# Two places and half transpositions for the planes of P, TensorE turns up to group 47, and an earlier load of x, in a macaron S4D block

## The chip, the cores and the metric

The kernel runs on one core of one Trainium2 chip. The metric is device time in microseconds (us) for one execution, the median of three runs. TensorE (PE) does the matmuls, VectorE (DVE), ScalarE (ACT) and GpSimd (POOL) the element-wise work, and SyncE (SP) issues most of the DMAs; ACT and POOL issue some too. Each engine works through its own queue in order.

## The reference

The input x is [8, 2048, 256] in float32: 8 sequences of 2048 tokens with 256 channels. A block of three sublayers is computed, each with a layer norm ahead of it and a residual after it:

```
x = x + 0.5 * ffn(layernorm(x))          # first feed-forward
x = x + s4d(layernorm(x))                # state-space convolution, with its own norm and skip
x = x + 0.5 * ffn(layernorm(x))          # second feed-forward, the same weights

ffn(v) = relu(v @ w1 + b1) @ w2 + b2     # 256 -> 1024 -> 256
K[h, l] = 2 Re sum_n Ct[h, n] exp(dtA[h, n] * l)      # 64 complex states for a channel
s4d(v) = layernorm(v + causal_conv(v, K) + v * D) * ln_w + ln_b
```

## The kernel before, in words

**Tiling.** The 16384 tokens are 128 blocks of 128, and two blocks make a group: there are 64 groups (`NG`). A feed-forward sublayer goes through the groups one after the other. Each group has eight slots (`SLOTS`), one for each 128 of the 1024 hidden channels. Values are split into a high and a low part, so in a slot `up` (L837) does six matmuls into `ph` and `down` (L848) six into `po`, the latter for the slot three before (`LAG`). Between them ACT takes the relu (L915) and DVE the low part (L916, shown as L116, since that is the helper's line). There are four buffers of `hx`.

**The order of the work.** `sublayer` (L862) counts steps t, one for each slot, from `-lead` on. In each step it writes the matmuls of a slot, and then calls `step()`, which advances every running generator by one `yield`. Generators are written as a number of yields before each action, so that the yields are the schedule. For group g, `pre` starts at step 8g - lead, and `post` at step 8g + 10. In `pre_a` (L966) the groups from 3 on load x into one of five slots of the tag `x` by a DMA that ACT issues (L971, pinned in ACT's order); the first three wait XL steps and load by SP. The statistics follow five steps after the load (`XY + 1`). The norm of a group's input and the norm of the output of the group three before are done together (`Joint`, L953).

**Turning the normalised tokens.** The first feed-forward matmul needs the channels on the partitions. Up to group 43 (`DMA_A = 44`) TensorE transposes four 128x128 blocks (L790), and ACT and DVE take the high and low part from PSUM (L799, L801). From group 44 on, `turn_by_dma` (L804) does it: DVE and ACT copy the low and the high 16-bit half of each number into two planes (L809), SP issues one DMA that transposes 16-bit blocks (L812), and DVE and ACT put the halves together again (L823), from which L825 and L827 take the high and low part. The planes, the turned planes and the result are tiles of the tag `pl`, which has two buffers of 2 KB for each partition.

**Making P in the background.** While the first sublayer runs, `matrices` (L257) makes the tables of the convolution as a background generator. It yields paces, and `fill` (L887) advances it whenever its sum of paces is behind the count of steps, of which each counts 1.32. The last part makes 32 tables P (`NBT`), each [128, 1024] in float32, in a pipeline of three parts, each with six sub-steps, over 9.1 units for the first 18 rounds and 10.3 after (`PA`, `PB_`):

- `make(bt)` (L586): six POOL operations write table bt.
- `spread(bt - 1)` (L612): in sub-steps 3 and 4, ACT copies the low and the high 16-bit halves of the table before into `planes` (L618); in sub-step 5, SP issues one DMA that transposes both planes, 16 blocks, into `turned` (L620); in sub-step 6 the table is stored as it is (L625).
- `transpose(bt - 2)` (L628): in sub-step 5, ahead of that DMA, DVE and ACT put the turned halves of the table before that together again (L635, `P_REINT`); in sub-step 6 the result is stored (L637).

So `planes` and `turned` are one place each: the copies of a table wait until the DMA of the table before has read `planes`, and the DMA waits until L635 has read `turned`. L618, L620 and L635 are pinned in the order of their queues.

**After the first sublayer.** The states are computed from P, scanned, and turned into outputs (`states`, `scan`, `outputs`), and the second feed-forward follows with the same code, in which all groups but two are turned by DMA (`DMA_B = 2`).

Of the kernel before, what the change touches and what calls it, by code (L numbers as in the profile page):

```python
# [13 lines left out]
U16 = mybir.dt.uint16  # L14
# [5 lines left out]
P = 128  # L20
# [23 lines left out]
def macaron_s4d_kernel(  # L44
# [17 lines left out]
    nc = tc.nc  # L62
    V = nc.vector
    A_ = nc.scalar
# [12 lines left out]
    TOK = NTB * P  # L77
    NG = NJ * B // NTB
    GPJ = B // NTB
    XL = 8  # L80
    LAGS_BEHIND = 3
    PIN = 1
    PINF = "a1", "a2"
# [2 lines left out]
    XY = 4  # L86
# [6 lines left out]
    BCH = 8  # L93
# [15 lines left out]
    def bank(tag, name):  # L109
        return ps.tile([P, 512], F32, name=name, tag=tag, bufs=BANKS[tag])  # L110

    def slot(tag, shape, name, dtype=F32):
        return work.tile(shape, dtype, name=name, tag=tag, bufs=BUFS[tag])

    def stt(o, a, s, b, op0, op1):
        return V.scalar_tensor_tensor(out=o, in0=a, scalar=s, in1=b, op0=op0, op1=op1)  # L116
# [19 lines left out]
    w1t, w2t = [wa1[:, i] for i in range(2)], [wa2[:, i] for i in range(2)]  # L136
# [15 lines left out]
    def load_weights():  # L152
        for _ in range(XL):
            yield
        pin = tc.keep_in_program_order
        q = W // 4
        raw1 = room[1][:, 0 : NDC * W].rearrange("p (i d f) -> p i d f", i=4, d=NDC)
        raw2 = room[1][:, NDC * W : NDC * W + NFC * H].rearrange("p (f m) -> p f m", m=H)
        at = NDC * W + NFC * H
        rows = [room[1][0:1, at + i * W : at + (i + 1) * W] for i in range(2)]  # L160
        ones = room[1][0:1, at + 2 * W : at + 2 * W + P]
        V.memset(ones, 1.0)
        nc.scalar.dma_start(out=rows[0], in_=w1[H - 1 : H])
        nc.scalar.dma_start(out=rows[1], in_=b1.rearrange("(o f) -> o f", o=1))

        spread_ = []

        def spread_rows(i):
            spread_.append([bank("ho"[i], f"spread{i}_{n}") for n in range(2)])
            for n in range(2):  # L170
                pin(nc.tensor.matmul(
                    spread_[i][n], ones, rows[n][:, i * 2 * q : (i + 1) * 2 * q],
                    start=True, stop=True,
                ))

        spread_rows(0)
        w2v = w2.rearrange("(fc p) m -> p fc m", p=P)
        for i in range(4):
            fs = slice(i * q, (i + 1) * q)
            W1Q[i].dma_start(  # L180
                out=raw1[:, i], in_=w1[:, fs].rearrange("(dc p) f -> p dc f", p=P)
            )
        for i in range(2):
            fs = slice(4 * i, 4 * i + 4)
            W2Q[i].dma_start(out=raw2[:, fs], in_=w2v[:, fs, :])
        for _ in range(7):
            yield
        for i in range(4):
            fs = slice(i * q, (i + 1) * q)
            hi = w1t[0][:, :, fs]  # L190
            last, bias = (b[:, i % 2 * q : (i % 2 + 1) * q] for b in spread_[i // 2])
            pin(V.tensor_sub(raw1[:, i], raw1[:, i], last.unsqueeze(1).to_broadcast([P, NDC, q])))
            pin(stt(raw1[:, i, NDC - 1], bias, ident[:, P - 1 : P], raw1[:, i, NDC - 1], ALU.mult, ALU.add))
            pin(A_.copy(hi, raw1[:, i]))  # L194
            pin(V.tensor_sub(w1t[1][:, :, fs], raw1[:, i], hi.bitcast(F32)))

            if i == 0:
                yield
                yield
                spread_rows(1)  # L200
            yield
        for i in range(4):
            fs = slice(2 * i, 2 * i + 2)
            hi = w2t[0][:, fs, :]
            pin(A_.activation(hi, raw2[:, fs], AF.Copy, scale=0.5))
            pin(stt(w2t[1][:, fs, :], raw2[:, fs], 0.5, hi.bitcast(F32), ALU.mult, ALU.subtract))
            yield
        for i in range(2):
            nc.sync.dma_start(out=w1_dram[i], in_=w1t[i].bitcast(F32))
            nc.sync.dma_start(out=w2_dram[i], in_=w2t[i].bitcast(F32))  # L210
# [46 lines left out]
    def matrices():  # L257
# [73 lines left out]
        f, a = r, z  # L331
# [29 lines left out]
        for k in range(1, 4):  # L361
# [14 lines left out]
        er, qr, qi, den, ta, tb, c2r, c2i, cr, ci, aa, ab, big, fa, fb, v, s, tt, g, e, mm_ = (  # L376
            cells[18:39]
        )
# [86 lines left out]
        for i in range(H // P):  # L465
            nc.gpsimd.dma_start(
                out=kpad[i * P : (i + 1) * P, P + 1 :], in_=zeros[:, 0 : P - 1]
# [6 lines left out]
        with nc.allow_non_contiguous_dma(reason="256 numbers"):  # L474
            nc.gpsimd.dma_start(
                out=kpad.rearrange("(g c) k -> c g k", c=2)[:, :, P], in_=k0
# [100 lines left out]
        def p_of(bt):  # L577

            r, i = (room[2], 28 + bt % 4 * 8) if bt < first else (room[3], (16, 24, 48, 56)[bt % 4])
            return r[:, i * P : (i + 8) * P]  # L580
# [31 lines left out]
        def spread(bt):  # L612

            pu = p_of(bt).bitcast(U16).rearrange("p (m w) -> p w m", w=2)
            yield
            yield
            for w in range(2):
                tc.keep_in_program_order(A_.copy(planes[:, w], pu[:, w]))  # L618
                yield
            tc.keep_in_program_order(nc.sync.dma_start(  # L620
                out=turned.rearrange("p w (k n) -> p (w k) n", n=P),
                in_=planes.rearrange("p w m -> p (w m)"), transpose=True,
            ))
            yield
            nc.sync.dma_start(out=o_dram[bt], in_=p_of(bt))  # L625
            yield
# [14 lines left out]
        planes, turned = both[:, 0], both[:, 1]  # L641
# [189 lines left out]
    XF = "pl"  # L831
    DEINT = (0, V.tensor_copy), (1, A_.copy)
    REINT = (0, V.tensor_copy), (1, A_.copy)
    DMA_A = 44
    DMA_B = 2

    def up(wt, xT, ph, fc):  # L837
# [125 lines left out]
    JG = 3  # L963
    P_MADE = 10, 46

    def pre_a(g):  # L966
        by_dma = g >= DMA_A
        for _ in range(XL if g < JG else 0):
            yield
        xt = xts[g] = slot("x", [P, NTB, H], f"xa_{g}")  # L970
        ins = (nc.scalar if g >= JG else nc.sync).dma_start(out=xt, in_=hbm(x, g))  # L971
        if g >= JG:
            tc.keep_in_program_order(ins)
        for _ in range(XY if g < JG else XY + 1):
            yield
        if g >= JG:
            joints[g - JG] = Joint(g - JG, by_dma)
        return (yield from ffn_in(xt, f"a{g}", NTB, by_dma, joints.get(g - JG)))
# [202 lines left out]
    def early():  # L1181

        xs = states_of(0)
        todo = list(batches(0))
        for j0, j1, pace in ((0, JE, 4.0), (JE, NJ - 1, 1.6)):
            while posted[0] < j1 * GPJ:
                yield 1.3
            n = (j1 - j0) * B
            per = min(512 // (2 * n), PB)
            for p0, bt in batches(0):  # L1190
                for l0 in range(0, PB, per):
                    pv = bank("b", f"pe{j0}_{bt}_{l0}")[:, 0 : 2 * per * n]
                    pv = pv.rearrange("p (r l m) -> p r l m", r=2, l=per)
                    for lb in range(l0, l0 + per, 2):
                        pts = []
                        for c in range(2):
                            pt = slot(("e", "te")[c], [P, 2, P], f"pe{bt}_{c}_{lb}_{j0}")
                            nc.sync.dma_start(
                                out=pt,
                                in_=pt_dram[bt].rearrange("k (c l m) -> k c l m", c=2, m=P)[:, c, lb : lb + 2],  # L1200
                            )
                            pts.append(pt)
                        yield pace
                        for l in range(lb, lb + 2):
                            for ri in range(2):
                                for c in range(2):
                                    nc.tensor.matmul(
                                        pv[c * N : (c + 1) * N, ri, l - l0, :],
                                        pts[c][:, l - lb, ri * N : (ri + 1) * N],
                                        some(j0, j1)[:, :, BCH * bt + 2 * l + c, :],  # L1210
                                        start=True, stop=True, skip_group_check=True,
                                    )
                        yield pace
                    keep(
                        xs, [pv[:, ri] for ri in range(2)], slice(p0 + l0, p0 + l0 + per),
                        slice((j0 + 1) * B, (j1 + 1) * B),
                    )
                    yield 1.3
            for _ in scan(0, G_, 0, sizes[0], max(j0, 1), j1, ("te", "e")):
                yield pace  # L1220
# [6 lines left out]
    def begin():  # L1227
        for _ in range(sizes[1] // PB):
            next(head)

    sublayer(
        w1t, w2t, pre_a, post_a, 19, "a", load_weights(), chain(matrices(), early()),
        {"half": NG // 2, "tables": NG * 3 // 4},
        {NG * SLOTS - 6: lambda: next(head), NG * SLOTS - 1: begin},
    )
# [126 lines left out]
```

## Time and profile before

| | |
|---|---|
| median of 3 runs | 1758.88 us (1758.41 to 1759.29) |
| the profiled execution | 1759.33 us, of which the span is 1757.4 us |
| busy: PE, DVE, ACT, POOL | 1723.9, 1378.7, 987.8, 587.8 us |
| first matmul of the states | 804 us |
| L618, copies into `planes` (ACT) | 64, 1046 ns at the median, from 221.1 to 580.7 us |
| L620, transposing DMAs of P (SP) | 32, landing 4.7 us after issue at the median |
| L635, copies out of `turned` | 32 on ACT of 1374 ns, 32 on DVE of 1285 ns at the median |
| L790, transposes of the first sublayer on PE | 176 |
| L812, transposing DMAs of the first sublayer | 20, landing 3.1 us after issue at the median |
| L971, loads of x by ACT | 61, landing 2.9 us after issue at the median |

How to read it: "L853 PE MATMUL po_a<-wa,hx_a" is an instruction of line 853 on TensorE that writes `po_a` from `wa` and `hx_a`; the suffix a is the first sublayer, b the second. A bracket behind an entry of a timeline is the time for which the engine was idle before it, and what ended that. In the rows of waits the three numbers are the total in us, the number of waits and the longest. In the windows each engine has its busy time and, in brackets, its instructions; behind them stand TensorE's granted clock (1.00 is full), the busy share of the DMA engines, and GB/s. In a tile's view three numbers with slashes are the shortest, the median and the longest duration in ns. SPq and ACTq are the queues of those engines, where DMAs are issued.

### The profile page before, as it was taken

What the parts mean: (1) busy time and instruction counts of PE and PEld (TensorE: products, weight loads), DVE (VectorE), ACT (ScalarE), POOL (GpSimd) and SP (SyncE); (2) the same over time, 40 slices, a digit from 0 to 9 for tenths busy, and PEclk for the clock granted to TensorE, in tenths of its full rate; (3) what the DMA queues carried; (4) which work ended last, traced back from release to release, by engine and by line L of the source; (5) the groups of instructions that cost most, each with busy time, mean ns of one, the idle gap of its engine ahead of it and who ended that gap; (6) DMA issues with size and microseconds to landing.
All of it is one profiled execution on the core that took longest, in us unless ns stands there. A gap on an engine that the chain in (4) does not pass through costs nothing.

```text
span 1757.4 us, 40914 instructions
## 1 busy us (share of the span) xinstructions
PE 1723.9 (98%) x15367; PEld 1696.8 (97%) x15367; DVE 1378.7 (78%) x4729; ACT 987.8 (56%) x2178; POOL 587.8 (33%) x550
## 2 busy tenths in 40 slices
PE   9999999999999999999999799999999999999998
PEld 7999999989999999999999799999999999999998
DVE  6998776676777767766999788888877888888884
ACT  4555476677777755544555445555455555555553
POOL 1117988886775105111000122222222222222220
PEclk9999999999999999999999999999999999999999
DMA  5111166566666533236888922222222222222321
GB/s 189 48 39 52 49 187 154 162 196 200 191 163 189 132 84 68 73 91 195 262 266 257 278 44 68 71 73 70 66 70 68 72 72 68 67 67 73 73 67 37
DMA packets 276861, 204.40 MB, mean 116 GB/s; under 512 B 162740, under 2 KB 235188, under 8 KB 276150
## 3 DMA queue, kind: packets, MB, share of 16 engines
q1 hardware_dynamic: 249232, 168.08, 35.6%
q10 hardware_dynamic: 26502, 32.52, 5.8%
q8 instruction: 120, 1.97, 0.5%
q0 software_dynamic: 928, 1.19, 0.4%
q14 instruction: 79, 0.65, 0.1%
HBM read 91.89 MB, written 71.57 MB: 93 GB/s over the span
## 4 chain that ended last, share of the span: by engine, by line
PE 71%; DVE 6%; DMA 4%; ACT 1%; issue 1%; POOL 0%; ACTq 0%; SPq 0%; DVEq 0%
PE ph_b L843 21%; PE po_b L853 21%; PE po_a L853 11%; PE ph_a L843 11%; PE pv L1089 2%; PE py L1164 2%; PE py L1155 2%; DMA planes<-planes 2%; DMA xa<-in_L_attn_x_dram 1%; DVE e L1119 1%; DVE te L1120 1%; DVE xsB L1122 1%; DMA pt<-pt 1%; DVE xsB L1121 1%; PE pt_a L790 0%
## 5 line engine op out<-in xcount | busy, mean ns | idle before, releaser
L853 PE MATMUL po_a<-wa,hx_a 128*128 128x256 f32 x3072 | 454.4, 285 | 11.9 <-DVE hx_a L116 11.9
L843 PE MATMUL ph_a<-xh_a,wa 128*128 128x256 f32 x2048 | 456.9, 287 | 0.7 <-ACT xh_a L799 0.7
L843 PE MATMUL ph_b<-xh_b,wb 128*128 128x256 f32 x2048 | 443.5, 284 | 0.7 <-ACT xh_b L799 0.7
L853 PE MATMUL po_b<-wb,hx_b 128*128 128x256 f32 x3072 | 441.6, 283 | 0.0
L853 PEld LDWEIGHTS po_a<-wa,hx_a 128*128 128x128 f32 x3072 | 405.1, 192 | 14.5 <-DVE hx_a L116 12.9
L853 PEld LDWEIGHTS po_b<-wb,hx_b 128*128 128x128 f32 x3072 | 401.1, 192 | 0.0
L843 PEld LDWEIGHTS ph_a<-xh_a,wa 128*128 128x128 f32 x2048 | 355.6, 193 | 3.8 <-ACT wa L194 1.5
L843 PEld LDWEIGHTS ph_b<-xh_b,wb 128*128 128x128 f32 x2048 | 353.3, 193 | 1.3 <-ACT xh_b L799 1.1
L915 ACT ACTIVATE hx_b<-ph_b 128x256 fp32r<-128x256 f32 x512 | 190.9, 383 | 259.6 <-PE ph_b L843 237.8
L915 ACT ACTIVATE hx_a<-ph_a 128x256 fp32r<-128x256 f32 x512 | 193.7, 387 | 228.5 <-PE ph_a L843 211.1
L116 DVE SCALAR_TENSOR_TENSOR hx_a<-ph_a,hx_a 128x256 fp32r<-128x256 f32 x512 | 208.9, 414 | 122.6 <-ACT hx_a L915 121.0
L843 PE MATMUL ph_a<-xl_a,wa 128*128 128x256 f32 x1024 | 290.6, 285 | 0.0
L843 PE MATMUL ph_b<-xl_b,wb 128*128 128x256 f32 x1024 | 285.5, 284 | 0.0
L116 DVE SCALAR_TENSOR_TENSOR hx_b<-ph_b,hx_b 128x256 fp32r<-128x256 f32 x512 | 210.1, 413 | 64.0 <-ACT hx_b L915 60.5
L1297 POOL TENSOR_TENSOR xb<-xb,lnb_sb 128x512 f32<-128x512 f32 x64 | 82.8, 1296 | 466.8 <-DMA xb<-x_dram 146.9
L843 PEld LDWEIGHTS ph_a<-xl_a,wa 128*128 128x128 f32 x1024 | 197.6, 193 | 0.6 <-DVE xl_a L801 0.4
L843 PEld LDWEIGHTS ph_b<-xl_b,wb 128*128 128x128 f32 x1024 | 197.7, 193 | 0.0
L773 POOL TENSOR_TENSOR xa<-xa,hb 128x512 f32<-128x512 f32 x64 | 85.0, 1328 | 288.0 <-ACT xn L726 283.8
L773 POOL TENSOR_TENSOR xb<-xb,hb 128x512 f32<-128x512 f32 x64 | 94.3, 1473 | 90.7 <-issue 58.7
L726 ACT ACTIVATE xn<-xb,nb_fb,t_fb 128x255 f32<-128x255 f32 x127 | 69.4, 594 | 89.0 <-DVE nb_fb L116 88.9
L726 ACT ACTIVATE u<-xa,nb_u,t_u 128x256 f32<-128x256 f32 x104 | 90.0, 865 | 0.0
L809 DVE COPY pl_b<-xn 128x512 uint16<-128x512 uint16 x62 | 27.1, 438 | 74.7 <-ACT xn L726 74.7
(266 smaller groups left out, 2553.3 us busy)
## 6 DMA issues: line engine op xcount, KB each, us to landing
o<-u SPq DMA_DIRECT2D x32, 512.0 KB, 4.0
pt<-u SPq DMA_DIRECT2D x32, 512.0 KB, 4.2
tz<-kpad SPq DMA_DIRECT2D x64, 256.0 KB, 4.6
xb<-x_dram SPq DMA_DIRECT2D x64, 256.0 KB, 2.7
out_dram<-xb SPq DMA_DIRECT2D x64, 256.0 KB, 2.9
x_dram<-xa ACTq DMA_DIRECT2D x62, 256.0 KB, 2.1
xa<-in_L_attn_x_dram ACTq DMA_DIRECT2D x61, 256.0 KB, 2.9
pt<-pt SPq DMA_DIRECT2D x60, 256.0 KB, 3.8
```

Source lines behind the costliest of these rows:

```text
L116: return V.scalar_tensor_tensor(out=o, in0=a, scalar=s, in1=b, op0=op0, op1=op1)
L726: ins = A_.activation(dst, src, AF.Identity, bias=nb[:, i : i + 1], scale=rs[:, i : i + 1])
L773: return G_.tensor_add(xt, xt, hb2.unsqueeze(1).to_broadcast([P, NTB, H]))
L809: copy(pl[:, w], xu[:, :, :, :, w])
L843: nc.tensor.matmul(ph, wt[wp][:, dc, fs], xp[:, dc, :], start=(n == 0), stop=(n == 3 * NDC - 1))
L853: nc.tensor.matmul(po[:, i, :], hp[:, tsl], wt[wp][:, fc, :], start=(fc == 0 and i == 0 and n == 0), stop=(fc == NFC - 1 and n == 2), skip ...
L915: last[A_] = A_.activation(hh, ph, AF.Relu)
L1089: ins = nc.tensor.matmul(pv[ri][c * N : (c + 1) * N, l, j0 * B : j1 * B], pts[c][:, l, ri * N : (ri + 1) * N], some(j0, j1)[:, :, BCH * bt ...
L1119: E.tensor_mul(t1, xv[:, :, :, j, :], wr_b)
L1155: nc.tensor.matmul(py[c][:, l, :], ucs[c][:, l, :], tzs[c][:, l, :], start=(l == 0), stop=False, skip_group_check=True,)
L1164: nc.tensor.matmul(py[c][:, l, :], xs[cs, ri, p0 + l, :], ots[ri][cs, l, :], start=False, stop=(l == PB - 1 and ri == 1), skip_group_check ...
L1297: G_.tensor_add(xt, xt, lnb_sb.unsqueeze(1).to_broadcast([P, NTB, H]))
```

## The change

Four things are changed.

- The planes of P lie in two places by turns. An even table uses `planes` as before; an odd table uses two half tiles of the tag `pl`, one for each plane.
- Each plane is turned by a DMA of its own, so that a table has two transposing DMAs of 8 blocks instead of one of 16. `turned` stays one tile, of which each DMA writes one half.
- `DMA_A` goes from 44 to 48: groups 44 to 47 of the first sublayer are turned by TensorE. As the tables are made by then, the tag `pl` isn't used by both.
- `lead` of the first sublayer goes from 19 to 20, XL from 8 to 9 and the yields behind a load from `XY + 1` to `XY + 2`: from group 3 on, the load of x stands one step earlier in ACT's order, and the statistics stand where they were.

```diff
-    XL = 8
+    XL = 9
...
             pu = p_of(bt).bitcast(U16).rearrange("p (m w) -> p w m", w=2)
+
+            if bt % 2:
+                halves_ = [slot("pl", [P, BCH * P], f"half{bt}_{w}", U16) for w in range(2)]
+            else:
+                halves_ = [planes[:, w] for w in range(2)]
             yield
             yield
             for w in range(2):
-                tc.keep_in_program_order(A_.copy(planes[:, w], pu[:, w]))
+                tc.keep_in_program_order(A_.copy(halves_[w], pu[:, w]))
                 yield
-            tc.keep_in_program_order(nc.sync.dma_start(
-                out=turned.rearrange("p w (k n) -> p (w k) n", n=P),
-                in_=planes.rearrange("p w m -> p (w m)"), transpose=True,
-            ))
+            for w in range(2):
+                tc.keep_in_program_order(nc.sync.dma_start(
+                    out=turned[:, w].rearrange("p (k n) -> p k n", n=P),
+                    in_=halves_[w], transpose=True,
+                ))
...
-    DMA_A = 44
+    DMA_A = 48
...
-        for _ in range(XY if g < JG else XY + 1):
+        for _ in range(XY if g < JG else XY + 2):
...
-        w1t, w2t, pre_a, post_a, 19, "a", load_weights(), chain(matrices(), early()),
+        w1t, w2t, pre_a, post_a, 20, "a", load_weights(), chain(matrices(), early()),
```

## The prediction

> **What bounds the kernel now.** I read the busy shares and the 40 slices first, then TensorE's waits, its timeline around each wait, the windows of 20 us for the same stretch, and last the waits of ScalarE (ACT) and the tile view of the planes.
>
> ```profile
> PE 1723.9 (98%) x15367; PEld 1696.8 (97%) x15367; DVE 1378.7 (78%) x4729; ACT 987.8 (56%) x2178; POOL 587.8 (33%) x550
> ...
> PE   9999999999999999999999799999999999999998
> ```
>
> TensorE is the bound, so an added matmul costs its full time, and a stall elsewhere counts only once it reaches TensorE. In the first sublayer that happens through one door; the waits give us in total, times, longest:
>
> ```profile
> PE po_a L853 <- DVE hx_a L116: 11.9, 9, 2.9
> ```
>
> ```profile
> 287.48 0.74 PE L853 MATMUL po_a<-wa,hx_a 128*128 128x256 f32 x4 [1.51 <-DVE hx_a L116]
> ...
> 341.77 0.98 PE L853 MATMUL po_a<-wa,hx_a 128*128 128x256 f32 x6 [1.84 <-DVE hx_a L116]
> 349.42 0.98 PE L853 MATMUL po_a<-wa,hx_a 128*128 128x256 f32 x6 [1.22 <-DVE hx_a L116]
> ...
> 394.62 0.98 PE L853 MATMUL po_a<-wa,hx_a 128*128 128x256 f32 x6 [2.92 <-DVE hx_a L116]
> ...
> 580.34 0.97 PE L853 MATMUL po_a<-wa,hx_a 128*128 128x256 f32 x6 [1.77 <-DVE hx_a L116]
> ```
>
> The bracket is the idle time. The other four are at 305.27 (0.53), 356.47 (0.95), 358.51 (0.35) and 566.84 (0.78). All nine lie between 280 and 600 us, most of the stretch in which P is made (221 to 594 us). Each has a tail: the first six po_a after it take 0.98 us where six take 0.72 in the chain, so 0.26 x 9 = 2.3 us. The longest one also costs clock:
>
> ```profile
> 340.00:360.00 20.00, 15.72 (x125) 15.09 (x125) 13.73 (x45) 15.56 (x29) 13.35 (x15) 1.00 0.78 200
> ...
> 380.00:400.00 20.00, 17.08 (x131) 16.88 (x130) 13.57 (x40) 13.61 (x24) 18.38 (x15) 0.91 0.82 222
> 400.00:420.00 20.00, 20.00 (x169) 20.00 (x168) 13.72 (x55) 17.05 (x30) 11.63 (x10) 1.00 0.75 228
> ```
>
> PE busy and its count stand second, the granted clock next to last but two. A clock of 0.91 over 20 us is 1.8 us lost. So 11.9 + 2.3 + 1.8 = 16.0 us. The counts say the same: against 170 matmuls in a full window, the seven short ones lack 14 + 7 + 2 + 45 + 39 + 23 + 6 = 136, at 20/170 = 0.118 us each 16.0 us. **That is all that this change can win.**
>
> What is behind the nine? ScalarE and VectorE (DVE) run in order, and while one waits at a P copy, the relus that feed TensorE stand behind it.
>
> ```profile
> ACT planes L618 <- DMA planes<-planes: 19.7, 15, 3.6
> ...
> ACT u L635 <- DMA planes<-planes: 4.1, 3, 2.2
> ```
>
> ```profile
> 337.79 1.99 ACT L618 COPY planes<-u 128x1024 uint16<-128x1024 uint16 x2 [3.64 <-DMA planes<-planes]
> ```
>
> ```profile
> 337.81 1.32 DVE L635 COPY u<-planes 128x1024 uint16<-128x1024 uint16 x1 [3.12 <-DMA planes<-planes]
> ...
> 578.21 0.75 DVE L675 BATCH_NORM_STATS2 st_fa<-xa 128x6 f32<-128x256 f32 x2 [3.90 <-DMA xa<-in_L_attn_x_dram]
> ```
>
> The chain of waits names the transfers (start, duration):
>
> ```profile
> 331.13 6.56 DMA planes<-planes
> ...
> 570.48 7.71 DMA xa<-in_L_attn_x_dram
> ```
>
> By the last wait ahead of each: five stalls hang on the planes' transposition (305.27, 341.77, 349.42, 356.47, 358.51: 4.89 us), three on x (287.48, 566.84, 580.34: 4.06 us), and 394.62 (2.92 us) on both, first 1.59 us of ACT at L635, then x, whose issue stood behind that.
>
> **The change, part by part.**
>
> *Two places.* L618 waits because the transposition of the batch before still reads `planes`. With places by turns it needs the one two batches back. A batch takes 9.1/1.32 of a step's time: a group with TensorE turns lasts 374.75 - 362.79 = 11.96 us, 1.495 a step, so 10.3 us up to the 18th batch (10.3/1.32 steps, 11.7 us, after). The largest landing is 8.8 us, so all 15 waits go (19.7 us of ACT). The odd halves take the tag `pl`, which no other tile uses until group 48. What is late next is L635, which still waits for its own transposition, and `turned` still has one place. But L635 of a batch comes two sub-steps of 10.3/6 after the L618 that stopped, 3.4 us, about the longest wait of 3.64.
>
> *Halves.* A half has the shape of the transposition of a group:
>
> ```profile
> L620 SPq DMA_TRANSPOSE planes<-planes x32: 1317/2028/4379, 223.2 to 583.3; - x32
> ...
> DMA to landing us min/median/max: 4.3/4.7/8.8
> ```
>
> ```profile
> L812 SPq DMA_TRANSPOSE pt_a<-pl_a x20: 1232/1232/1292, 551.9 to 778.8; - x20
> ...
> DMA to landing us min/median/max: 3.0/3.1/4.5
> ```
>
> The first half can be issued after the first copy of 1.05 us and lands in 3.1: 4.7 + 1.05 - 3.1 = 2.6 us sooner for VectorE's copy. The second is issued 1.23 later and lands 4.3 after the first: 1.4 us sooner for ScalarE's. The price is 2 x 1.23 - 2.03 = 0.43 us of SyncE's queue in each batch, hidden: queued behind on SP are only the stores of o and pt, which no engine waits for at that point (x is issued by ACT). If crowding stretches an issue to the row's 4.38, the second half lands up to 4.38 - 1.23 = 3.2 us later than so reckoned, 1.8 later than now. I take the median rows, since a half is the nearest shape, and keep the other end for the range.
> The Trainium skill speaks against this part: "DMA: Bandwidth & Descriptors", "Rules for kernel authors", says to coalesce small transfers, and its fit (in "Anatomy of one DMA") has about 2.0 us fixed for each. By that the second half would land some 2 us after the whole one, the stalls at 341.77, 356.47, 358.51 and 394.62 would stay (6.06 + 4 x 0.26 + 1.8 = 8.9 us), and the sum below would be some 1759 us. The rows (3.1 for half, 4.7 for all) show 1.6 us for the second half instead.
>
> *x a step sooner.* A step is 12 matmuls, 1.44 us in the chain. Reading, `lead` 19 to 20 and XL 8 to 9 cancel for the first three groups and the weights (steps -11, -3, 5; -11), and XY + 2 leaves the statistics where they were. What moves is one ACT-issued DMA per group (0.39 us of queue), now ahead of the store of the group before instead of just after it (570.08 and 570.48). Its slot was last read by the normalisation two steps before, so it should add no wait. Each of the three x stalls shrinks by at most 1.44: 1.44 + 0.78 + 1.44 = 3.66. An issue comes sooner only if ACT gets there, so I take 2.6. Below nothing is possible if x now meets the transposition, as at 279.25, where one issued 1.9 us earlier goes with a landing of 7.08; that end goes into the range.
>
> *Groups 44 to 47 by TensorE.* 16 more transposes. Periods: 11.96 with them, 597.87 - 586.35 = 11.52 by DMA. So 4 x 0.44 = **1.76 us added**, certain since nothing hides it. Gone are four transpositions from SP and, per group, 0.62 + 0.77 us on ACT and 0.68 + 0.45 less xl's equal share on DVE, just where 566.84 and 580.34 stall.
>
> **Sum.** Of the planes' five I take 4.5 of 4.89, of 394.62 2.2 of 2.92 (its ACT wait of 1.59 by the half's 1.4, its x by the step), of x's 2.6: 9.3 us. Seven tails 1.8, the clock 1.8: 12.9 won. Against it 1.76, and for the L635 waits that now end last two stalls of the present mean (11.9/9 + 0.26 = 1.6): 3.2. Net 7.9. The profiled execution took 1759.33 (span 1757.4 and 1.9 around it), giving 1751.4; it lies 0.45 above the median 1758.88, so **1751**.
>
> **The rivals.**
> *The wait moves.* L618's wait reappears at L635, because `turned` has one place and the transposition itself is no shorter; only x and its three stalls gain (2.6 + 0.8), less 1.76: about 1757. For it: 12.2 us of DVE waits at L635 already, 8 of them. Against: both halves come sooner. That the change does nothing lies here too: the copies are pinned in ACT's order, and if that order puts them no earlier, the freed place is unused.
> *Halves crowd the queues (slower).* Place: between 280 and 400 us, with DMA shares of 0.5 to 0.8. If an issue takes 4.4 us as the row's longest does, a batch is L635 (1.4) + 4.4 + 4.7 = 10.5 us, and from 10.3 on the copies fall behind in every batch. One stall of 1.6 in ten of the first 18 batches is 16, with 1.76, and 6 of the old ones cured: about 1771. Against: the issue's median of 2.03 for the whole.
>
> **Chances.** Forecast (1745 to 1755.4) 0.68, the wait moves (1755.4 to 1762.4) 0.16, slower 0.16. A measurement of this kernel can tell about 0.2% (3.5 us) from no change. Low end: all 16.0 won less 1.76 gives 1744.7. High end: 1762, where the crowded queue begins; some 0.03 lie below and 0.13 above.
>
> **What would show it.** Right: L618 has no waits on the DMA; po_a's waits fall from 11.9 to 2 to 5 us; no clock below 1.00 at 380 to 400; pt_a by TensorE has 192 transposes; a planes half lands in some 3 us. Wrong: DVE's and ACT's waits at L635 above their 16.3 us together, x landings above 7 us still ahead of st_fa, new po_a waits after 400 us, where there are none to 560.

## The result, and the profile after

The changed kernel takes 1764.17 us (median of 13 runs, 1759.88 to 1768.63), the kernel before beside it 1757.09 us (13 runs, 1754.20 to 1763.05): a ratio of 1.0035 with a 95% interval of 1.0024 to 1.0045. It is slower, by 6 us by the ratio and 7 by the medians, where 8 us less were forecast. The profiled execution took 1762.85 us, its span is 1760.7 us, 3.3 more than before, so the two traces show half of the loss. Lines behind L614 have moved down by five or six: L618 is now L623, L620 L626, L635 L641, L853 L859, L971 L977.

The busy time of TensorE and its slices, from the page of the changed kernel:

```profile
PE 1724.7 (98%) x15383; PEld 1696.4 (96%) x15383; DVE 1375.5 (78%) x4721; ACT 983.1 (56%) x2170; POOL 591.2 (34%) x550
...
PE   8999999999999999999999899999999999999998
```

TensorE has 16 instructions more, the transposes of groups 44 to 47, and still bounds the kernel. Its waits and those of its suppliers (total, times, longest):

```profile
DVE st_fa L681 <- DMA xa<-in_L_attn_x_dram: 32.3, 33, 3.2
ACT xn L732 <- DVE nb_u L119: 21.2, 17, 3.1
...
PE po_a L859 <- DVE hx_a L116: 9.5, 11, 2.1
...
ACT u L641 <- DMA planes<-planes: 6.0, 3, 2.8
...
DVE u L641 <- DMA planes<-planes: 3.1, 1, 3.1
```

Three of these rows before the change:

```profile
DVE st_fa L675 <- DMA xa<-in_L_attn_x_dram: 29.3, 33, 3.9
...
DVE u L635 <- DMA planes<-planes: 12.2, 8, 3.1
...
ACT xn L726 <- DVE nb_u L119: 9.1, 11, 1.4
```

ACT's 19.7 us at the copies into the planes have no row left at all. DVE's wait for its own transposition fell from 12.2 to 3.1 us, and 1.3 more for a half. But ACT's normalisation `xn` now waits 21.2 us for DVE's shift `nb_u`, where it was 9.1 us. The prediction doesn't speak of that row. The windows of 20 us of the changed kernel (PE busy and its count stand second, the clock next to last but two):

```profile
20.00:40.00 20.00, 19.10 (x154) 18.24 (x152) 13.38 (x56) 8.81 (x23) 1.27 (x1) 1.00 0.66 251
40.00:60.00 20.00, 17.44 (x141) 16.81 (x142) 15.46 (x59) 10.76 (x24) 3.87 (x3) 1.00 0.13 41
140.00:160.00 20.00, 17.93 (x149) 17.37 (x148) 19.35 (x45) 9.58 (x23) 17.91 (x21) 1.00 0.19 41
...
340.00:360.00 20.00, 18.01 (x145) 17.26 (x144) 16.20 (x56) 15.79 (x26) 15.89 (x16) 1.00 0.88 256
...
380.00:400.00 20.00, 20.00 (x170) 20.00 (x169) 14.33 (x59) 16.77 (x31) 16.23 (x15) 1.00 0.82 229
```

The stretch that the prediction looked at is better: 340 to 360 lacks 25 matmuls instead of 45, and 380 to 400 none, at full clock. But the first three windows held 159, 167 and 167 before. Counted as the prediction counted, against 170 matmuls in every window and at 0.118 us each, with the first `pv` (the first matmul of the states) beside it:

| profiled execution | lacking 20 to 220 us | lacking 220 to 600 us | first `pv` | `pv` to second feed-forward | the rest |
|---|---|---|---|---|---|
| before | 21 | 139 | 804.0 | 207.2 | 746.2 |
| after | 75 (+6.4 us) | 95 (-5.2 us) | 805.6 | 209.9 | 745.1 |
| without the x part (below) | 22 (+0.1 us) | 53 (-10.1 us) | 796.3 | 210.8 | 745.4 |

Up to the first `pv` the changed kernel loses 6.4 and gains 5.2 by these counts, which hold what the clock costs, and the 16 transposes are 1.8 us of added work: 3.0 us in all, where 1.6 were measured. (In the last row 10.0 less 1.8 makes 8.2 won, and 7.7 arrive at the first `pv`.) So the count is good to some 1.5 us, and the loss has two sides: the start, in which nothing of P is made, became worse, and the stretch of P gained half of what it gains without the earlier load of x.

**The first three groups.** SyncE's queue in the changed kernel:

```profile
4.36 1.43 SPq L977 DMA_DIRECT2D xa<-in_L_attn_x_dram  x1
20.44 1.06 SPq L209 DMA_DIRECT2D w_dram<-wa  x2
22.03 2.10 SPq L210 DMA_DIRECT2D w_dram<-wa  x2
24.18 1.24 SPq L977 DMA_DIRECT2D xa<-in_L_attn_x_dram  x1
```

The load of group 2 stands behind four stores of the weights. Before, it was the second of an entry of two, ahead of them:

```profile
4.36 3.18 SPq L971 DMA_DIRECT2D xa<-in_L_attn_x_dram  x2
```

DVE and TensorE pay for the late load (the timelines of both after the change):

```profile
35.08 0.75 DVE L681 BATCH_NORM_STATS2 st_fa<-xa 128x6 f32<-128x256 f32 x2 [1.62 <-DMA xa<-in_L_attn_x_dram]
```

```profile
40.04 0.33 PE L796 MATMUL pt_a<-ident,xn 128*128 128x128 f32 x1 [0.26 <-ACT xn L732]
40.53 0.55 PE L796 MATMUL pt_a<-ident,xn 128*128 128x128 f32 x3 [0.16 <-ACT xn L732]
41.75 0.74 PE L849 MATMUL ph_a<-xh_a,wa 128*128 128x256 f32 x4 [0.67 <-ACT xh_a L805]
44.17 0.38 PE L849 MATMUL ph_a<-xl_a,wa 128*128 128x256 f32 x1 [1.69 <-DVE xl_a L807]
```

Issued at 24.18, the load is there at 35.05, 10.87 us later. TensorE idles step by step as the late group reaches it: transposes, high part, low part. The windows 20 to 60 lack 31 matmuls more than before, 3.7 us.

**The statistics.** One place some 490 us on, as DVE, ACT and TensorE show it:

```profile
525.95 0.17 DVE L703 RECIPROCAL t_u<-s_u 128x4 f32<-128x4 f32 x1
528.48 0.75 DVE L681 BATCH_NORM_STATS2 st_fa<-xa 128x6 f32<-128x256 f32 x2 [2.36 <-DMA xa<-in_L_attn_x_dram]
...
531.23 0.58 DVE L119 TENSOR_SCALAR nb_u<-mv_j,t_u 128x1 f32<-128x1 f32 x4
```

```profile
531.48 1.09 ACT L732 ACTIVATE xn<-xa,nb_u,t_u 128x255 f32<-128x255 f32 x2 [3.11 <-DVE nb_u L119]
```

```profile
529.97 0.98 PE L859 MATMUL po_a<-wa,hx_a 128*128 128x256 f32 x6 [0.59 <-DVE hx_a L116]
```

`t_u` and `nb_u` belong to one group's norm, `st_fa` to the next group, whose x has only just been asked for. It stands in the middle of that norm, DVE waits 2.36 us for x with `nb_u` (and an `hx_a`) queued behind it, and ACT waits 3.11 us. By the order of DVE's instructions in the traces, `st_fa` of the next group is ahead of `nb_u` in 13 of 60 groups before, and in 45 of 60 after.

### The profile page after: what moved, and what is told of

Same layout as the page of the kernel before. It is cut to its first block, busy times and chain, and to the rows that moved or that the text cites. A ratio compares the mean times of both kernels' runs of the same rounds, so it can differ in the third digit from the quotient of the medians.

```text
span 1760.7 us, 40998 instructions
## 1 busy us (share of the span) xinstructions
PE 1724.7 (98%) x15383; PEld 1696.4 (96%) x15383; DVE 1375.5 (78%) x4721; ACT 983.1 (56%) x2170; POOL 591.2 (34%) x550
## 3 DMA queue, kind: packets, MB, share of 16 engines
q0 software_dynamic: 928, 1.19, 0.4%
## 4 chain that ended last, share of the span: by engine, by line
PE 89%; DMA 4%; DVE 3%; ACT 1%; issue 1%; SPq 0%; ACTq 0%; DVEq 0%
PE po_b L859 21%; PE ph_b L849 21%; PE po_a L859 18%; PE ph_a L849 18%; PE py L1170 3%; PE py L1161 3%; PE pv L1095 3%; DMA xa<-in_L_attn_x_dram 2%; PE pt_a L796 1%; DVE u L641 1%; DMA planes<-half 1%; DMA planes<-planes 1%; DMA pt<-pt 1%; DMA wb<-w_dram 1%; DVE hx_a L116 0%
## 5 line engine op out<-in xcount | busy, mean ns | idle before, releaser
L859 PE MATMUL po_a<-wa,hx_a 128*128 128x256 f32 x3072 | 455.6, 285 | 9.6 <-DVE hx_a L116 9.5
L859 PE MATMUL po_b<-wb,hx_b 128*128 128x256 f32 x3072 | 441.3, 283 | 0.5 <-DVE hx_b L116 0.5
L859 PEld LDWEIGHTS po_a<-wa,hx_a 128*128 128x128 f32 x3072 | 404.9, 192 | 12.9 <-DVE hx_a L116 12.2
L859 PEld LDWEIGHTS po_b<-wb,hx_b 128*128 128x128 f32 x3072 | 400.5, 192 | 1.0 <-DVE hx_b L116 0.9
```

The source lines that it names most:

```text
L859: nc.tensor.matmul(po[:, i, :], hp[:, tsl], wt[wp][:, fc, :], start=(fc == 0 and i == 0 and n == 0), stop=(fc == NFC - 1 and n == 2), skip ...
```

## The experiments

**Theory.** The parts on the planes do what was reckoned. The x part loses more than they win, in two ways: group 2 is loaded late, and the planner, which orders DVE's unpinned instructions, draws the statistics forward behind the earlier load. The second way was added after the first four runs below, whose expectations speak of the late group 2 alone. **Rivals:** the halves crowd the queues; turning groups 44 to 47 costs more than priced; an earlier load collides with the transpositions as such. Each kernel was timed in five rounds beside the kernel before, whose median in the four sessions was 1758.58 (the first four runs), 1758.03 (the next four), 1758.50 (the next four) and 1757.34 us. 0.001 in a ratio is 1.76 us; the intervals are some 2 us to either side, so differences of 1 to 3 us between two experiments are told by their medians alone. Where two experiments of different sessions are compared below, the times are not corrected for the 1.5 us by which the medians of the kernel before differ.

**Only the x part.** In the kernel before:

```diff
-    XL = 8
+    XL = 9
...
-        for _ in range(XY if g < JG else XY + 1):
+        for _ in range(XY if g < JG else XY + 2):
...
-        w1t, w2t, pre_a, post_a, 19, "a", load_weights(), chain(matrices(), early()),
+        w1t, w2t, pre_a, post_a, 20, "a", load_weights(), chain(matrices(), early()),
```

> Only the load of x a step sooner (lead 20, XL 9, XY + 2); planes in one place, turned whole, group 44 the first turned by DMA. Theory 'late group 2': group 3's load now stands a step ahead of group 2's, and so SyncE issues group 2's load behind the four stores of the split weights; it lands some 10 us after issue, and TensorE loses 4 to 6 us before 60 us of the span. So 3 to 6 us slower than the kernel before. Rival 'halves crowd the queues': this kernel has none of it, 1 to 3 us faster. Rival 'TensorE turns and what the planner makes of them': not here either, 1 to 3 us faster.

Measured 1776.34 us, 1.0105 (1.0092 to 1.0118). This alone loses 17.8 us, more than the whole change, and three times what the late group 2 was expected to cost.

**Everything but the x part.** The change, with these three edits taken back (XL 8, XY + 1, lead 19):

```diff
-    XL = 9
+    XL = 8
```

> Two places, halves and group 48, without the earlier load of x. 'Late group 2': no stall before 60 us, the stalls by the planes are mostly gone; 1 to 4 us faster than before. 'Halves crowd the queues': 4 to 10 us slower, with waits at the copies out of the turned planes. 'TensorE turns and the planner': 2 to 5 us slower, lost after 800 us of the span.

Measured 1752.97 us, 0.9969 (0.9957 to 0.9981): 5.6 us faster than before, more than was expected, and 11.2 less than the change. The waits of this kernel:

```profile
DVE st_fa L681 <- DMA xa<-in_L_attn_x_dram: 32.5, 37, 2.9
...
ACT xn L732 <- DVE nb_u L119: 7.5, 10, 1.4
...
PE po_a L859 <- DVE hx_a L116: 2.7, 6, 0.8
```

DVE waits for x about as often and as long as in the changed kernel (32.5 and 32.3 us), and TensorE hardly notices. What differs is what stands behind the wait. One such wait in DVE's timeline, first in this kernel, then in the one with the x part alone (the statistics that wait, and the shift of the group before them):

```profile
411.46 0.58 DVE L119 TENSOR_SCALAR nb_u<-mv_j,t_u 128x1 f32<-128x1 f32 x4
413.77 0.75 DVE L681 BATCH_NORM_STATS2 st_fa<-xa 128x6 f32<-128x256 f32 x2 [1.73 <-DMA xa<-in_L_attn_x_dram]
```

```profile
414.83 0.75 DVE L681 BATCH_NORM_STATS2 st_fa<-xa 128x6 f32<-128x256 f32 x2 [3.03 <-DMA xa<-in_L_attn_x_dram]
...
418.81 0.58 DVE L119 TENSOR_SCALAR nb_u<-mv_j,t_u 128x1 f32<-128x1 f32 x4
```

Shift first, and TensorE idles 0.19 us at 415.10. Statistics first, and it idles 1.73 us at 416.03. The count of groups with the statistics first is 14 of 60 here, 44 with the x part alone.

**Group 2 back in its place,** in the whole change. Groups 0 to 2 load one step sooner, so that group 2 is again not behind group 3:

```diff
-        for _ in range(XL if g < JG else 0):
+        for _ in range(XL - 1 if g < JG else 0):
...
-        for _ in range(XY if g < JG else XY + 2):
+        for _ in range(XY + 1 if g < JG else XY + 2):
```

> The whole change, but the first three groups wait XL - 1 steps and have XY + 1 yields behind the load, so that group 2's load stands ahead of group 3's again and SyncE issues it ahead of the weight stores. 'Late group 2': 4 to 6 us faster than the changed kernel, so 0 to 4 us faster than before. 'Halves crowd the queues' and 'TensorE turns and the planner': as slow as the changed kernel, 5 to 8 us slower than before.

Measured 1762.24 us, 1.0021 (1.0008 to 1.0033). The window 40 to 60 has its 167 matmuls again, but the gain is only 1.9 us where 4 to 6 were expected, and in the profiled execution the first `pv` comes later, at 809.0. So the late group 2 isn't the main cause. Statistics first: still 46 of 60.

**Only the groups 44 to 47,** in the kernel before:

```diff
-    DMA_A = 44
+    DMA_A = 48
```

> Only groups 44 to 47 turned by TensorE. By the 16 transposes 1.8 us slower than before, less up to 2.5 us for the two stalls at 566 and 580 us that the DMA turns took part in: between 1 us faster and 2 us slower by 'late group 2' and by 'halves crowd the queues'. 'TensorE turns and the planner': 3 to 6 us slower, with the loss after 800 us of the span.

Measured 1758.92 us, 1.0005 (0.9997 to 1.0014). This rival falls: 0.3 us, transposes and what they cure together.

**The statistics pinned,** in the whole change, in DVE's order at the place where the program has them:

```diff
-            stats(halves(xt), f"f{name}", mv=joint.mv[:, 0:NTB])
+            stats(halves(xt), f"f{name}", True, joint.mv[:, 0:NTB])
```

> The whole change, with the statistics of a joint group's x pinned in DVE's order at the place where the program has them (six steps behind the load, and behind the shift nb_u of the group before). Theory 'statistics ahead of the shift': the planner put them one or two slots behind the earlier load, ahead of nb_u of the group before in 45 of 60 groups (13 before the change), so DVE's wait for x delays nb_u, ACT's xn and the relus behind it; pinned, DVE's waits for x (32.3 us) and ACT's for nb_u (21.2 us) fall below 10 us, and the kernel is 6 to 11 us faster than the changed one, 1753 to 1758; the late load of group 2 is still there. Rival 'an earlier load collides on the DMA queues or in ACT's order': the waits for x stay and the time stays at 1761 to 1766.

Measured 1756.40 us, 0.9992 (0.9982 to 1.0002), where the change is at 1.0035. Its waits:

```profile
ACT xn L732 <- DVE nb_u L119: 7.4, 9, 1.8
...
DVE st_fa L681 <- DMA xa<-in_L_attn_x_dram: 4.1, 2, 2.6
```

With no group's statistics ahead of the shift, ACT's row is back at 7.4 us. This one word in the program is worth 7.8 us by the medians. Of the 6.1 us between the profiled executions, 2.9 lie ahead of the first `pv` and 2.9 behind it, in a stage that the pin doesn't touch (more on that at the end of the next section).

**Pinned, and group 2 in its place** (both edits above):

```diff
+        for _ in range(XL - 1 if g < JG else 0):
...
+            stats(halves(xt), f"f{name}", True, joint.mv[:, 0:NTB])
```

> The same, and group 2's load ahead of group 3's as in the third experiment. 'Statistics ahead of the shift' and the late group 2 as a second, smaller cost: 2 to 4 us faster than with the pin alone, 1749 to 1755, faster than the kernel before. Rival 'an earlier load collides': 1759 to 1764.

Measured 1754.99 us, 0.9985 (0.9976 to 0.9993), the upper end of what was expected, and 1.4 us below the one before where 2 to 4 were expected.

**Pinned, without the x part,** which asks whether the pin is a gain in itself:

```diff
-    XL = 9
+    XL = 8
...
+            stats(halves(xt), f"f{name}", True, joint.mv[:, 0:NTB])
```

> Two places, halves and group 48, the load of x where it was, and the statistics pinned. 'Statistics ahead of the shift': DVE's waits for x (32.5 us without the pin) nearly vanish; 0 to 4 us faster than the second experiment, 1749 to 1753. Rival 'an earlier load collides': the pin changes nothing, 1753.

Measured 1761.86 us, 1.0019 (1.0009 to 1.0029): a miss. That the pin is no gain in itself was expected, a loss of 8.9 us was not. One thing that it adds is a wait of ACT's root:

```profile
ACT s_u L692 <- DVE mv_j L685: 15.2, 19, 4.1
```

Without the pin it is 2.6 us in 3 waits. But the whole change with the same pin has this wait too, 15.0 us in 20 waits, and is 5.5 us faster than this kernel, so it isn't shown as the cause. What differs more between the two is ACT's wait at the copies L641, 14.0 us here and 7.8 there, the longest of 5.34:

```profile
369.34 1.33 ACT L641 COPY u<-planes 128x1024 uint16<-128x1024 uint16 x1 [5.34 <-DMA planes<-half]
```

How the pin and the later load bring that about was not tried.

**One place, halves and groups 44 to 47,** without the x part:

```diff
+            halves_ = [planes[:, w] for w in range(2)]
...
-    XL = 9
+    XL = 8
```

> Halves and group 48, but the planes in one place, the load of x where it was. If the second place is what frees ACT, ACT's waits at the copies into the planes stay near half of their 19.7 us (the halves come 1.6 to 2.6 us sooner) and the time lies between 1755 and 1758; if the halves alone do it, 1753 as in the second experiment; if the halves cost and the places pay, 1759 to 1762.

Measured 1755.48 us, 0.9984 (0.9974 to 0.9995). The copies still wait for the planes, half of the 19.7 us:

```profile
ACT planes L623 <- DMA planes<-planes: 10.2, 7, 4.1
```

The second place brings the next 2.5 us, by the medians; the intervals overlap.

**The x part alone, with both repairs.** The statistics are pinned four steps behind their load, two sooner than the program has them, and group 2 is in its place:

```diff
-        for _ in range(XL if g < JG else 0):
+        for _ in range(XL - 1 if g < JG else 0):
...
-        for _ in range(XY if g < JG else XY + 2):
+        for n in range(XY + 1 if g < JG else XY + 2):
+            if g >= JG and n == 4:
+                joints[g - JG] = Joint(g - JG, by_dma)
+                stats(halves(xt), f"fa{g}", True, joints[g - JG].mv[:, 0:NTB])
             yield
...
-            stats(halves(xt), f"f{name}", mv=joint.mv[:, 0:NTB])
```

> The load of x a step sooner alone, as in the first experiment (17.8 us slower than before there), with two repairs: group 2's load ahead of group 3's, and the statistics pinned four steps behind the load, so that they stand ahead of the shift nb_u of the group before in 2 of 60 groups instead of 44. Theory 'statistics ahead of the shift, and the late group 2': the loss goes, 1755 to 1760, and no stall before 60 us. Rival 'an earlier load collides on the DMA queues or in ACT's order': the load is as early as in the first experiment, 1770 to 1778.

Measured 1759.06 us, 1.0004 (0.9991 to 1.0017). The 17.8 us are gone though the load is as early, so that rival falls: an earlier load by itself doesn't cost them. It wins nothing that can be seen either. Statistics first: 2 of 60.

**The whole change with these repairs:**

```diff
+            if g >= JG and n == 4:
+                joints[g - JG] = Joint(g - JG, by_dma)
+                stats(halves(xt), f"fa{g}", True, joints[g - JG].mv[:, 0:NTB])
```

> The whole change with the same two repairs (6 of 60 groups instead of 45). Theory: the gain of the planes stays and x costs nothing, 1750 to 1755, as good as the second experiment (1753.0) or better by the 1 to 2 us that a step sooner may be worth. Rival 'an earlier load collides': 1759 to 1764.

Measured 1755.69 us, 0.9982 (0.9970 to 0.9994): 8.5 us less than the change, but repaired, too, the x part shows no gain over the change without it (0.9969).

**Without the x part, pinned three steps behind the load,** again two sooner than the program has them:

```diff
-    XL = 9
+    XL = 8
...
+            if g >= JG and n == 3:
+                joints[g - JG] = Joint(g - JG, by_dma)
+                stats(halves(xt), f"fa{g}", True, joints[g - JG].mv[:, 0:NTB])
```

> Two places, halves and group 48, x where it was, the statistics pinned three steps behind the load instead of five. The fifth-step pin lost 9 us against no pin (1761.9 to 1753.0), at stalls where ACT stood at the copies out of the turned planes. If that was the price of late statistics (the root waits for them: 15.2 us on ACT), two steps sooner gives most of it back, 1752 to 1756; if any pin upsets the planner's order, 1759 to 1763.

Measured 1756.53 us, 0.9988 (0.9976 to 0.9999). By the medians the pin costs 3.6 us instead of 8.9, and the root waits 4.1 us instead of 15.2; of the three places tried here, the planner's own is the best.

**Only the halves,** one place, in the kernel before:

```diff
+            for w in range(2):
+                tc.keep_in_program_order(nc.sync.dma_start(
+                    out=turned[:, w].rearrange("p (k n) -> p k n", n=P),
+                    in_=planes[:, w], transpose=True,
+                ))
```

> Only the halves: one place, group 44, x where it was. By the runs so far (halves with group 48: 1755.5; group 48 alone: 1758.9) between 1754 and 1758. If the halves crowd the queues beside the DMA turns of groups 44 to 47, 1759 to 1763.

Measured 1759.10 us, 1.0003 (0.9993 to 1.0014), above what was expected and at the lower edge of what was set down for crowded queues, so this time alone doesn't decide between the two. The trace speaks against crowding: an issue takes 1.30 us at the median, L623 waits 6.9 us in 4 waits instead of 19.7, and L641 waits 13.4 us (ACT and DVE together) instead of 16.3; and the kernels with halves and group 48 above are faster than before. But alone these shorter waits win nothing.

**The x part alone, with one repair each.** Group 2 in its place only:

```diff
-        for _ in range(XL if g < JG else 0):
+        for _ in range(XL - 1 if g < JG else 0):
```

> The load of x a step sooner alone, with only group 2's load put ahead again; the statistics stand ahead of the shift in 45 of 60 groups, as without repair. If the statistics are the greater cause (7.8 us to 1.9 us by the repairs of the whole change): 3 to 5 us off the 1776.3, so 1771 to 1774. If the late group 2 is, 1759 to 1764.

Measured 1767.91 us, 1.0056 (1.0043 to 1.0069), between the two ranges that were expected; statistics first in 45 of 60. And the statistics pinned four steps behind the load, group 2 left late:

```diff
+            if g >= JG and n == 4:
+                joints[g - JG] = Joint(g - JG, by_dma)
+                stats(halves(xt), f"fa{g}", True, joints[g - JG].mv[:, 0:NTB])
```

> The load of x a step sooner alone, with only the statistics pinned four steps behind the load (ahead of the shift in 2 of 60 groups); group 2's load is still behind the weight stores. If the statistics are the greater cause: 1760 to 1764, with the stalls before 60 us of the span still there. If the late group 2 is, 1770 to 1776.

Measured 1761.63 us, 1.0015 (1.0006 to 1.0025); 2 of 60. With the x part alone, the four cases stand against before so:

| us against before | group 2 late | group 2 in its place |
|---|---|---|
| statistics left to the planner | +17.8 | +10.6 |
| statistics pinned | +4.3 | +0.6 |

The 95% intervals of the four are 16 to 21, 8 to 12, 1 to 4 and -2 to 3 us. The statistics are worth 10.0 to 13.5 us, group 2 is worth 7.2 beside the unpinned statistics and 3.7, within the noise, beside the pinned ones. The start tells the same: with the statistics unpinned the windows 20 to 60 hold 295 matmuls with group 2 late and 326 with it in its place, 3.7 us apart; with the pin they hold 307 and 310, so there the pin itself keeps the start short, and the late load costs little of it.

## Why the prediction was wrong

The sign was wrong, through one step that was taken as reading and not as cost.

- **The two places: right.** "all 15 waits go (19.7 us of ACT)": no such row is left. The sum had 7.9 net; less 2.6 for x and the tails of its three stalls (0.8), 4.5 are left for the rest. Without the x part the medians show 5.6 us won, and in the profiled execution the first `pv` came 7.7 us sooner (804.0 to 796.3).
- **The halves: right in size.** The changed kernel's tile view of the planes:

```profile
L626 SPq DMA_TRANSPOSE planes<-planes x32: 1232/1281/2576, 228.0 to 574.9; - x32
...
DMA to landing us min/median/max: 3.1/3.8/7.4
```

  The issue takes 1.28 us (1.23 taken) with 3.05 at most in the other place (4.38 feared), and the landing is 3.8 against 4.7 for both planes in one. DVE's and ACT's waits at L641 are 12.0 us together, from 16.3. The halves bring time only with something else beside them: nothing alone (0.6 us of loss, within the noise), 2.5 gained with `DMA_A = 48`, and 2.5 more with the second place. The fit that the prediction set against this part stands on its page for DMAs that GpSimd issues; these are issued by SP, and two of them cost nothing that can be seen against one.
- **Groups 44 to 47: nothing speaks against the price.** 1.76 us was called certain; 0.3 was measured (-0.5 to 2.5 us), but that is net. With `DMA_A = 48` alone the windows 560 to 600 hold 333 matmuls instead of 311, which is 2.6 us of cured stalls against the price. In the changed kernel the two stalls at 566.84 and 580.34 are gone (169 and 170 matmuls in these windows).
- **The failed step: x a step sooner.** "`lead` 19 to 20 and XL 8 to 9 cancel for the first three groups and the weights (steps -11, -3, 5; -11), and XY + 2 leaves the statistics where they were. What moves is one ACT-issued DMA per group". Both halves of this hold for the program and not for the queues. Step 5 for group 2 is the old step, but group 3's load went from 5 to 4, so group 2 is now behind it. In SP's queue group 2's load then came behind the stores of the weights. And of the x part only the load is pinned. The statistics are written at the same step, but by DVE's order they came about 1.2 steps earlier in the mean, and in 45 of 60 groups ahead of the shift of the group before: apparently the planner puts them where it reckons x to be there. Taken at 2.6 us won, the x part cost 11.2 within the change, 9.4 of it ahead of the first `pv` in the profiled executions.
- **The range of that step was looked for at the wrong end.** The loss was bounded by x meeting the transposition on the DMA engines. The rows of before already showed the other price: `st_fa` waited 29.3 us there, and only the order of 47 of 60 groups kept that from ACT.
- **The rivals.** The wait did not move to L641, and the queues were not crowded. The slower side came by a mechanism that was not among them, so its 0.16 gets no credit from the result.

What stays open: between the first `pv` and the second feed-forward the profiled executions of all these kernels spend 206.3 to 211.4 us, in no clear relation to the edits. So 2.7 us of the change's loss, and 3.6 us that the kernel without the x part gave back of its 7.7, lie in a stage that no edit touches. The four that spend 209.9 us and more (the change, it without the x part, it with both repairs, and the pin three steps behind the load) are just those in which TensorE's clock is halved for 3.4 us some 186 us behind the first `pv`, of which 1.7 are lost; whether the replanned order or chance brings that about was not settled. The stall of 2.07 us at 159.13 comes with the place of the statistics: the window 140 to 160 holds 136 to 157 matmuls in the eleven kernels with the x part or a pin, and 166 or 167 in the five with neither. That is 1.2 to 3.7 us, which no repair took back, and how it comes about was not tried. The version with the lowest median is the change without the x part, 1752.97 us; its interval overlaps with those of the repaired changes.

## What to carry to other kernels

Where a planner orders an engine's queue, a load that is moved can take unpinned readers with it: ask for each reader whether it is pinned, and what it will stand ahead of. A wait in an in-order queue is priced by what is queued behind it and not by its length: 32.5 us of waits for x cost almost nothing in one order, and 32.3 us cost some 8 us in another. When several counts are changed so that they cancel, check the order between the parts that were compared with each other (group 2 and group 3), and not only each part's own step.

## What the runs showed of the hardware

**A short idle can halve the clock, and needn't.** In windows of 1 us of the changed kernel, after an idle of 2.10 us that ends at 990.37:

```profile
990.00:991.00 1.00, 0.49 (x4) 0.30 (x4) 0.93 (x4) 0.00 (x0) 0.00 (x0) 1.00 1.11 329
991.00:992.00 1.00, 0.93 (x10) 0.93 (x12) 0.96 (x4) 0.00 (x0) 0.00 (x0) 0.65 1.07 357
992.00:993.00 1.00, 1.00 (x14) 1.00 (x14) 0.93 (x5) 0.00 (x0) 0.00 (x0) 0.50 0.67 192
993.00:994.00 1.00, 1.00 (x12) 0.96 (x10) 0.93 (x5) 0.00 (x0) 0.00 (x0) 0.50 0.09 30
994.00:995.00 1.00, 1.00 (x9) 0.82 (x6) 0.42 (x2) 0.72 (x2) 0.30 (x1) 0.65 0.14 33
```

Idles of 1.95 us (the pinned change, at 366.78) and 2.15 us (the change with group 2 in its place, at 156.28) did the same, and in that last run one of 1.65 us (at 827.26); 2.82 us (x alone, at 366.89) brought half clock for 7 us. An idle of 2.07 us (at 159.13 after the change), one of 1.84 us before it, and one of 2.39 us (group 2 in its place, at 423.86) did not. The Trainium skill, "TensorE: Matmul & The Clock Gate", "Why this matters for your kernels", allows gaps of up to some 3 us; here gaps of 1.65 to 2.15 us were enough in four cases, so the measurement decides.

**A load behind stores is slow.** The 256 KB of x landed 10.87 us after their issue behind 4 MB of stores, at a DMA share of 0.88 (24 to 35 us), against 2.8 us at the median of the loads on ACT.

**DVE stands still beside POOL.** The timelines of DVE and POOL in the changed kernel:

```profile
364.92 3.98 DVE L641 COPY u<-planes 128x1024 uint16<-128x1024 uint16 x1 [1.15 <-DMA planes<-half]
```

```profile
363.72 1.29 POOL L603 TENSOR_TENSOR u<-u 128x512 f32<-128x512 f32 x1
364.98 1.05 POOL L599 TENSOR_TENSOR u<-u 128x512 f32<-128x512 f32 x1
366.00 1.05 POOL L605 TENSOR_TENSOR u<-u 128x512 f32<-128x512 f32 x1
367.01 1.28 POOL L603 TENSOR_TENSOR u<-u 128x512 f32<-128x512 f32 x1
```

The copy takes 0.74 us at its shortest and 3.98 here, in which POOL runs without a break, and TensorE idles 1.52 us right behind it, at 369.85. In the traces before and after, eleven of the twelve copies beside which POOL runs nothing take 0.73 to 0.78 us (the other 1.19), and those beside POOL up to 4.34. The Trainium skill, "SBUF — State Buffer", "SBUF: two separate sides", calls the port pair that the two share an exclusive lock for a whole instruction, for DVE operations of certain kinds; the rows agree with one engine waiting for the other, though the trace doesn't tell of which kind the copy is, and no run here took POOL's work away.
